# Summing the first quarter of each Strassen product in PSUM, in a four-layer graph network

## The chip, the cores and the metric

The kernel runs on one core of one Trainium2 chip. The metric is the device time of one execution in microseconds (us). The core has five engines with a queue each: TensorE (PE in the profile, with its weight loads as PEld) multiplies and writes to PSUM, an accumulator memory of eight banks of 512 float32 columns on 128 partitions; VectorE (DVE) and ScalarE (ACT) read and write PSUM and the working memory SBUF; GpSimd (POOL) works on SBUF alone; SyncE (SP) issues most of the transfers to and from DRAM.

## What is computed

128 graphs of 128 nodes with 512 features, x, and a matrix of edge weights, adj, for each graph, go through four layers. Each ends in `x = _layernorm(x + layer(x))`, which subtracts the mean over the 512 features and divides by the standard deviation. All is in float32.

- Layer 0: a transition matrix is made from adj and two scores of each node; the result is relu(x W0 + T x W1 + T T x W2 + biases).
- Layer 1: two hypergraph convolutions (512 to 1024 to 512 features), with a relu and a layer norm on the 1024 hidden features between them.
- Layer 2: an adjacency made from the sum of two node scores, row-normalised, times x, times a 512 x 512 weight.
- Layer 3: attention with 8 heads; the scores are multiplied by twice adj; then the output projection.

## The kernel before, in words

**Tiles.** Graphs go in pairs (`U = 2`), and two pairs (`both`) make one step of a layer, so a layer has 32 steps. A weight multiplication of a pair is done by one level of Strassen's scheme in Winograd's form, `strassen`: the left matrix (two graphs by the features) and the weight are cut in four, and seven products of sums of blocks take the place of eight. Where `twice` is used, a second level stands over it for two pairs: seven calls of `strassen`. A step has 29 calls: 7 in layer 0 (output width `nh` = `QW` = 386), 7 and 2 in layer 1, 2 in layer 2, 7 (queries and keys), 2 (values) and 2 (output) in layer 3, all of these 256 wide. In `twice`, two of the seven calls write fresh results; the other five add to what stands there, with `biased_take`.

**A call of `strassen`** uses three PSUM banks. `al` takes the product P1, then S2 T2 is added to it (step V), then S3 T3 (step C22), and at the end A22 N4 (step C21). `be` takes P5 (S1 T1), then S4 B22 (step C12). `ga` takes A12 B21 (step P2). After every one of the seven groups of matmuls a function of `take` reads the bank: `take["p1"]` copies P1 to the quarter d11, and `take["c11"]` adds P2 to it. In `plain_take` the first is a ScalarE copy and the second a VectorE addition; in `biased_take` both are VectorE's. A later group of matmuls on `al` waits until the reader before it is done. In `fresh` of layer 0 a read is split: ScalarE copies columns 128 on, VectorE adds a bias to the first 128.

**Layer norms.** `layer_norm` takes the statistics of one graph's rows (`bn_stats`), and `norm_terms` makes from them two columns: VectorE aggregates, adds eps to the variance and negates the mean; GpSimd raises the variance to the power -1/2 (`po.tensor_tensor(..., neghalf, OP.pow)`); ScalarE multiplies the negated mean by it. Then ScalarE applies both to the rows. There are 640 such norms.

**PSUM places.** Six places of the kind `bank` and one each of `t0` and `t1` fill the eight banks. `t0` and `t1` serve the T x steps of layer 0 (there too, ScalarE copies into PSUM and TensorE then adds to the copy, with `start=False`), and join `bank` when layer 0 no longer needs them.

**Order.** Nothing is ordered by loops. Every operation is recorded by `Plan.add` with a key (the layer's step plus the entries of `WHEN0`, `WHEN1`, `WHEN2` and the like), the operations that it depends on, and the tiles that it uses. `Plan.order` (line 250 on) then lists all engines' operations together: at each point an engine takes, of the operations that could start within `SLACK` of the soonest, the one of lowest rank, by durations from `estimate` and delays between engines from `LATENCY`. A tile gets a place when its first operation is listed; places of one kind are given in the order of a common line, and out of order only where at least four more are free. `Plan.emit` writes the order out. Since it issues all instructions itself, the profile puts every instruction on its line 373; groups are told apart by tiles and shapes. Waits between engines are put in afterwards, from what each instruction reads and writes.

**The end.** In `attention`, `last` marks the last pair of graphs: its probabilities are turned by TensorE (`pe.transpose` and a ScalarE copy), while those of all other pairs are written to DRAM by `through_dram` and read back, then turned by VectorE (`turned`).

Of the kernel before, what the change touches and what calls it, by code (L numbers as in the profile page):

```python
# [14 lines left out]
OP = mybir.AluOpType  # L15
AX = mybir.AxisListType

P = 128
# [14 lines left out]
OUTS = 3  # L33
SPACE = 3


# [31 lines left out]
SIZE = {"four": U * D, "sq": U * (P + 2), "bank": D, "col": 12, "row": D, "w28": 7168, "q7": 7 * 2 * P,  # L68
        "w7": 7 * QW, "out": U * 4 * QW, "t0": D, "t1": D, "row1": 4 * D, "k": U * (P + 2),
        "prep": U * D}  # L70

SIDE = 2
PSUM = "bank", "t0", "t1"

# [307 lines left out]
def kernel(  # L382
# [27 lines left out]
    slots = {"w7": 7, "out": OUTS, "q7": 0, "w28": 0, "sq": SQS, "col": COLS, "row": ROWS, "bank": 6, "t0": 1, "t1": 1,  # L410
             "four": BUFS, "row1": 0, "k": 0, "prep": 0}
    for kind in ("sq", "col", "row", "bank", "t0", "t1", "four"):
# [201 lines left out]
    def strassen(ops, W, nk, nh, take, more=None, flip=False):  # L614
# [21 lines left out]
        mm(al, A11, B11, True)  # L636
        take["p1"](al[:, :nh])
        be = bank()
# [3 lines left out]
        take["v"](al[:, :nh])  # L642
        ga = bank()
        mm(ga, A12, B21, True)
        if "c11" in more:
# [43 lines left out]

    def norm_terms(st, n=1):  # L690
        mv = col(2)
        ve.bn_aggr(mv, st[:, :6 * n])
        ve.tensor_scalar(mv[:, 1:2], mv[:, 1:2], EPS, None, op0=OP.add)
        ve.tensor_scalar(mv[:, 0:1], mv[:, 0:1], -1.0, None, op0=OP.mult)
        rstd = col(1)
        po.tensor_tensor(rstd, mv[:, 1:2], neghalf, OP.pow)
        nmr = col(1)
        ac.mul(nmr, mv[:, 0:1], rstd)
        return nmr, rstd

    def layer_norm(t):

        st = col(12)
        stats(st, 0, t)
        nmr, rstd = norm_terms(st)
        ac.activation(t, t, AF.Identity, bias=nmr, scale=rstd)

    def normed(take, t):

        def then(f, b):  # L710
            def run(p):
                f(p)
                layer_norm(t[:, b])
# [155 lines left out]
    def prepare0():  # L869
# [80 lines left out]
    def layer0(i0):  # L950
# [16 lines left out]
        def fresh(bs):  # L967
            def takes(d):
                def put(d, b):
                    def run(p):  # L970
                        ac.copy(d[:, P:], p[:, P:])
                        add(d[:, :P], p[:, :P], b, OP.add)
                    return run
                d11, d12, d21, d22 = d
                return plain_take(*d) | {"p1": put(d11, bs[:, 0]), "v": put(d12, bs[:, 1]),
                                         "p5": put(d22, bs[:, 1]), "c21": put(d21, bs[:, 0])}
            return takes
# [25 lines left out]
        for r, i in enumerate(both):  # L1003
            plan.key = base + WHENT[1][r]
            x0 = load_rows(x[i:i + U].rearrange("b p f -> p b f"))
            TT = pair_turned(loads[r])
            for m in (1, 0):
                for b in range(U):
# [5 lines left out]
                    if m:  # L1014
                        ac.copy(to, by)
                    else:
                        ve.scalar_tensor_tensor(x0[:, b], p, 0.0, x0[:, b], op0=OP.max, op1=OP.add)
                        layer_norm(x0[:, b])
                plan.key += .2
# [115 lines left out]
    def layer1(i0):  # L1135
# [66 lines left out]
        for r, i in enumerate(both):  # L1202
            plan.key = base + STEP1 * (5, 7)[r]
            for b in range(U):
# [4 lines left out]
                sts = col(12)  # L1209
                for g in range(2):  # L1210
                    stats(sts, g, h[r][b][:, g])
                nmr, rstd = norm_terms(sts, 2)
                ac.activation(t, t, AF.Identity, bias=nmr, scale=rstd)
                loads.append(through_dram(h[r][b].rearrange("p (j g) (k w) -> p j (g k) w", j=1, k=2), f"h{i + b}"))
        for r, i in enumerate(both):
# [14 lines left out]

            q = four()
            for b in range(U):
                ve.scalar_tensor_tensor(q[:, b], bw2, drds[r][:, b:b + 1], b2_b, op0=OP.mult, op1=OP.add)
                ve.scalar_tensor_tensor(q[:, b], x1[:, b], 2.0, q[:, b], op0=OP.mult, op1=OP.add)
            for b in range(U):
                p = bank()
                pe.matmul(p, K[:, b, :P], G[:, b], start=True, stop=True)
                ve.scalar_tensor_tensor(q[:, b], p, dns[r][b], q[:, b], op0=OP.mult, op1=OP.add)
                layer_norm(q[:, b])
            sp.dma_start(x2d[i // U], q)  # L1240
# [91 lines left out]
    def layer23(i0):  # L1332
# [64 lines left out]
        def fresh(bias):  # L1397
            def takes(d):
# [6 lines left out]
                d11, d12, d21, d22 = d  # L1405
                return plain_take(*d) | {"p1": put(d11, 0), "v": put(d12, 1), "p5": put(d22, 1), "c21": put(d21, 0)}
            return takes
# [144 lines left out]
```

## Time and profile before

| What | Value |
|---|---|
| Median of 3 runs | 5459.64 us (5459.48 to 5468.14) |
| Profiled execution | 5463.22 us; from its first to its last instruction (span) 5461.4 us |
| Instructions | 93,897 |
| TensorE busy | 5338.6 us, 98% of the span |
| VectorE busy | 4544.2 us, 83% |
| GpSimd busy | 4032.8 us, 74% |
| ScalarE busy | 2382.0 us, 44% |
| Mean granted TensorE clock | 0.994 of full |
| DRAM | 459.43 MB read, 350.09 MB written, 148 GB/s over the span |

A float32 matmul of the code is two records in the trace, and a transpose on TensorE too. Layer 0 takes the span from its start to about 1400 us, layer 1 goes to about 3100 us, layers 2 and 3 take the rest. How to read a group's line: engine, operation, the tile written, the tiles read, shapes, how many; then busy time in us and the mean of one in ns; then the idle time of the engine just before them, and who ended it. A line of waits has who waited, for whom, us in total, how often, and the longest. A line of a stretch has its ends and length, then each engine's busy time and instructions, the clock, and the share and rate of the transfers.

### The profile page before, as it was taken

To read this page: it belongs to the slowest core of one execution; us is meant where nothing else is said; L and a number is where in the kernel's file an instruction comes from. 1 tells how busy PE (TensorE), PEld (TensorE's weight loads), DVE (VectorE), ACT (ScalarE), POOL (GpSimd) and SP (SyncE) were. 2 spreads that over 40 slices of the span, in tenths; PEclk is the share of its full clock that TensorE was granted. 3 is DMA by queue.
4 is the path that set the end of the run, shared out by engine and by line. 5 is a ranking of instruction groups with operands and counts; after the bars stand their busy time and mean duration, and the time that the engine had idled before them with its cause. 6 is when DMAs were issued, how large, how long until landed. Compare 5 with 4: busy or idle time off the path is not lost.

```text
span 5461.4 us, 93897 instructions
## 1 busy us (share of the span) xinstructions
PE 5338.6 (98%) x29065; PEld 4256.9 (78%) x29065; DVE 4544.2 (83%) x11573; ACT 2382.0 (44%) x6437; POOL 4032.8 (74%) x4875
## 2 busy tenths in 40 slices
PE   8999999999999999999999999999999999999998
PEld 4555555555778888888888888998999998999987
DVE  6889888887888989998989878787787887787776
ACT  2434433344434444444444344554444444545444
POOL 6777777665777777777777567877777777777776
PEclk9999999999999999999999999999999999999999
DMA  3444444445454554554545645555555555455443
GB/s 100 134 139 125 133 143 128 128 120 162 146 149 150 145 155 150 151 157 147 154 146 150 225 139 159 167 155 157 162 154 164 156 158 161 153 163 162 153 153 123
DMA packets 841933, 815.80 MB, mean 149 GB/s; under 512 B 269388, under 2 KB 640596, under 8 KB 841431
## 3 DMA queue, kind: packets, MB, share of 16 engines
q1 hardware_dynamic: 839926, 807.18, 48.7%
q8 instruction: 230, 3.77, 0.3%
q10 hardware_dynamic: 1504, 2.62, 0.2%
q14 instruction: 273, 2.23, 0.1%
HBM read 459.43 MB, written 350.09 MB: 148 GB/s over the span
## 4 chain that ended last, share of the span: by engine, by line
PE 76%; DVE 10%; DMA 4%; POOL 3%; SPq 3%; issue 2%; ACT 1%; DVEq 0%; POOLq 0%; ACTq 0%
PE bank L373 58%; PE t L373 19%; DVE out L373 3%; DVE four L373 3%; SPq L373 3%; DVE col L373 2%; POOL four L373 1%; DVE side L373 1%; DMA sq<-in_adj_dram 1%; POOL out L373 1%; DMA first<-x3d 1%; DMA four<-in_x_dram 0%; DMA out<-x3d 0%; ACT out L373 0%; DVE sq L373 0%
## 5 line engine op out<-in xcount | busy, mean ns | idle before, releaser
L373 PE MATMUL bank<-first,four 128*128 128x386 f32 (+3 forms) x6114 | 1733.2, 430 | 58.4 <-DVE out L373 21.8
L373 PEld LDWEIGHTS bank<-first,four 128*128 128x128 f32 (+2 forms) x6114 | 1070.3, 189 | 640.1 <-DVE out L373 132.1
L373 DVE TENSOR_TENSOR out<-bank,out 128x386 f32<-128x386 f32 (+1 forms) x2030 | 981.6, 502 | 211.9 <-PE bank L373 164.2
L373 POOL TENSOR_TENSOR col<-col,neghalf 128x1 f32<-128x1 f32 x640 | 368.7, 582 | 452.1 <-DVE col L373 451.5
L373 DVE TENSOR_TENSOR four<-bank,four 128x256 f32<-128x256 f32 x1256 | 514.8, 416 | 177.5 <-PE bank L373 158.3
L373 POOL TENSOR_TENSOR out<-out 128x772 f32<-128x772 f32 (+3 forms) x250 | 350.2, 1408 | 263.2 <-DVE out L373 189.4
L373 PE MATMUL bank<-first,out 128*128 128x256 f32 (+2 forms) x2048 | 498.7, 377 | 7.5 <-DVE side L373 2.8
L373 POOL TENSOR_TENSOR four<-four 128x256 f32<-128x256 f32 (+2 forms) x439 | 357.6, 827 | 142.7 <-DVE four L373 76.1
L373 ACT COPY out<-bank 128x258 f32<-128x258 f32 (+2 forms) x527 | 214.1, 409 | 550.7 <-PE bank L373 414.2
L373 PEld LDWEIGHTS bank<-first,out 128*128 128x128 f32 (+2 forms) x2048 | 372.3, 189 | 77.3 <-issue 9.5
L373 POOL TENSOR_TENSOR four<-four,four 128x256 f32<-128x256 f32 (+2 forms) x479 | 414.0, 869 | 7.2 <-PE bank L373 1.3
L373 ACT ACTIVATE col<-col,col 128x1 f32<-128x1 f32 x640 | 183.9, 291 | 401.0 <-POOL col L373 348.5
L373 PE MATMUL bank<-first 128*128 128x128 f32 (+1 forms) x2356 | 329.6, 278 | 1.9 <-DVE four L373 1.3
L373 ACT ACTIVATE four<-four,col,col 128x512 f32<-128x512 f32 (+1 forms) x367 | 324.2, 887 | 7.4
L373 PEld LDWEIGHTS bank<-first 128*128 128x128 f32 (+1 forms) x2356 | 300.5, 189 | 18.1 <-issue 2.9
L373 PE MATMUL bank<-out,first 128*128 128x128 f32 (+2 forms) x1832 | 301.0, 305 | 1.1 <-DVE col L373 0.8
L373 ACT COPY four<-bank 128x256 f32<-128x256 f32 (+1 forms) x329 | 137.7, 422 | 355.5 <-PE bank L373 333.5
L373 DVE BATCH_NORM_STATS2 col<-four 128x6 f32<-128x512 f32 x430 | 287.6, 678 | 4.8 <-ACT four L373 3.1
L373 PEld LDWEIGHTS bank<-out,first 128*128 128x128 f32 (+1 forms) x1832 | 250.1, 187 | 19.4 <-issue 1.5
L373 PE MATMUL t<-out,sq 128*128 128x512 f32 x512 | 255.5, 594 | 6.4 <-DVE sq L373 2.5
L373 PE MATMUL bank<-four,first 128*128 128x256 f32 (+3 forms) x1424 | 253.3, 322 | 2.7 <-DVE first L373 1.1
L373 ACT COPY t<-out 128x512 f32<-128x512 f32 x256 | 151.0, 591 | 198.6 <-DVE four L373 107.2
(567 smaller groups left out, 12925.7 us busy)
## 6 DMA issues: line engine op xcount, KB each, us to landing
four<-x1d SPq DMA_DIRECT2D x69, 512.0 KB, 5.2
four<-h SPq DMA_DIRECT2D x66, 512.0 KB, 4.5
four<-in_x_dram SPq DMA_DIRECT2D x504, 64.0 KB, 2.1
h<-four SPq DMA_DIRECT2D x252, 128.0 KB, 2.6
four<-in_x_dram SPq DMA_DIRECT2D x60, 512.0 KB, 3.9
x1d<-four SPq DMA_DIRECT2D x60, 512.0 KB, 2.8
four<-S SPq DMA_DIRECT2D x50, 512.0 KB, 4.4
h<-out SPq DMA_DIRECT2D x188, 128.0 KB, 2.4
```

Source lines behind the costliest of these rows:

```text
L373: call(*map(real, args), **{n: real(a) for n, a in kw.items()})
```

## The change

**Strassen.** After P1, ScalarE copies it from `al` to the third bank, `ga`. The matmuls of P2 then go to `ga` with `start=False`, so that TensorE adds P2 to the copy. `take["p1"]` is gone, and `take["c11"]` is what `take["p1"]` was: it writes d11 in one read (a ScalarE copy in `plain_take`, one VectorE operation with the bias or the old contents in `biased_take`).

**PSUM places.** `ga` gets two places of its own, `g`, and `bank` keeps four. After layer 0 the 256-wide sums use halves of the first of these (`gh`), and the second joins `bank`. At the start every place that will be added to on top of a copy gets one matmul with `start=True`, two more than before.

**Layer norms.** The two graphs of a pair are taken together: one addition of eps on two columns, one power on two columns (GpSimd), and one product on VectorE in place of the negation there and the product on ScalarE. The norm of the first graph is applied when the statistics of the second are there.

**The end.** `last` now holds for the last two pairs.

```diff
+SEEDED = 2
-PSUM = "bank", "t0", "t1"
+PSUM = "bank", "g", "gh", "t0", "t1"
...
-    slots = {..., "bank": 6, "t0": 1, "t1": 1,
+    slots = {..., "bank": 6 - SEEDED, "g": SEEDED, "gh": 0, "t0": 1, "t1": 1,
...
+    places["gh"] = [places["g"][0][:, k * D // 2:(k + 1) * D // 2] for k in range(2)]
+    for k in range(2):
+        later["gh", k] = [("g", 0)]
+    later["bank", len(places["bank"])] = [("g", 1)]
+    places["bank"].append(places["g"][1])
...
         mm(al, A11, B11, True)
-        take["p1"](al[:, :nh])
+        ga = tile_of("g" if nh > D // 2 else "gh", nh)
+        ac.copy(ga[:, :nh], al[:, :nh])
...
-        ga = bank()
-        mm(ga, A12, B21, True)
+        mm(ga, A12, B21, False)
...
-            "p1": lambda p: ac.copy(d11, p), "c11": lambda p: add(d11, p, d11, OP.add),
+            "c11": lambda p: ac.copy(d11, p),
...
-            "p1": op(d11, b11, 0), "c11": op(d11, d11, 0), "v": op(d12, b12, 0), "c12": op(d12, d12, 0),
+            "c11": op(d11, b11, 0), "v": op(d12, b12, 0), "c12": op(d12, d12, 0),
...
+    def norm_terms(sts):
+        mv = col(2 * U)
+        for b, st in enumerate(sts):
+            ve.bn_aggr(mv[:, 2 * b:2 * b + 2], st)
+        mean, var = (mv.rearrange("p (b k) -> p k b", k=2)[:, k] for k in range(2))
+        ve.tensor_scalar(var, var, EPS, None, op0=OP.add)
+        rstd = col(U)
+        po.tensor_tensor(rstd, var, neghalf.to_broadcast([P, U]), OP.pow)
+        nmr = col(U)
+        ve.scalar_tensor_tensor(nmr, mean, -1.0, rstd, op0=OP.mult, op1=OP.mult)
+        return [(nmr[:, b:b + 1], rstd[:, b:b + 1]) for b in range(U)]
+    def layer_norms():
+        sts = []
+        def one_more(t):
+            sts.append((t, col(6)))
+            stats(sts[-1][1], 0, t)
+            if len(sts) == U:
+                for (t, _), (nmr, rstd) in zip(sts, norm_terms([st for _, st in sts])):
+                    ac.activation(t, t, AF.Identity, bias=nmr, scale=rstd)
+        return one_more
...
-        for kind in ("t0", "t1"):
-            p = tile_of(kind, D)
+        for kind, k in ("g", 0), ("g", 1), ("t0", 0), ("t1", 0):
+            p = tile_of(kind, D, place=k)
...
-        last = i0 + U == B
+        last = i0 + 2 * U >= B
```

More of the change, by code (lines that the diff above doesn't have):

```diff
@@ L68 @@
 SIZE = {"four": U * D, "sq": U * (P + 2), "bank": D, "col": 12, "row": D, "w28": 7168, "q7": 7 * 2 * P,
-        "w7": 7 * QW, "out": U * 4 * QW, "t0": D, "t1": D, "row1": 4 * D, "k": U * (P + 2),
+        "w7": 7 * QW, "out": U * 4 * QW, "t0": D, "t1": D, "g": D, "gh": D // 2, "row1": 4 * D, "k": U * (P + 2),
         "prep": U * D}
 SIDE = 2
-PSUM = "bank", "t0", "t1"
+PSUM = "bank", "g", "gh", "t0", "t1"
 class Tile:
@@ L409 @@
                                   if at("w7", i) < at(kind, k) + SIZE[kind] and at(kind, k) < at("w7", i) + SIZE["w7"]]
-    slots = {"w7": 7, "out": OUTS, "q7": 0, "w28": 0, "sq": SQS, "col": COLS, "row": ROWS, "bank": 6, "t0": 1, "t1": 1,
+    slots = {"w7": 7, "out": OUTS, "q7": 0, "w28": 0, "sq": SQS, "col": COLS, "row": ROWS, "bank": 6 - SEEDED, "g": SEEDED, "gh": 0, "t0": 1, "t1": 1,
              "four": BUFS, "row1": 0, "k": 0, "prep": 0}
-    for kind in ("sq", "col", "row", "bank", "t0", "t1", "four"):
+    for kind in ("sq", "col", "row", "bank", "g", "t0", "t1", "four"):
         places[kind] = [(psum if SIZE[kind] == D and kind != "row" else const).tile([P, SIZE[kind]], FP, name=f"{kind}{k}")
@@ L688, in stats @@
         ve.bn_stats(st[:, 6 * k:6 * k + 6], piece)
[L690 to L706, printed above, removed]
+    def norm_terms(sts):
[18 more added lines that the diff above has]
+        return one_more
     def normed(take, t):
+        norm = layer_norms()
         def then(f, b):
@@ L712, in run @@
                 f(p)
-                layer_norm(t[:, b])
+                norm(t[:, b])
             return run
@@ L974, in takes @@
                 d11, d12, d21, d22 = d
-                return plain_take(*d) | {"p1": put(d11, bs[:, 0]), "v": put(d12, bs[:, 1]),
+                return plain_take(*d) | {"c11": put(d11, bs[:, 0]), "v": put(d12, bs[:, 1]),
                                          "p5": put(d22, bs[:, 1]), "c21": put(d21, bs[:, 0])}
@@ L1006, in layer0 @@
             TT = pair_turned(loads[r])
+            norm = layer_norms()
             for m in (1, 0):
@@ L1017, in layer0 @@
                         ve.scalar_tensor_tensor(x0[:, b], p, 0.0, x0[:, b], op0=OP.max, op1=OP.add)
-                        layer_norm(x0[:, b])
+                        norm(x0[:, b])
                 plan.key += .2
@@ L1203, in layer1 @@
             plan.key = base + STEP1 * (5, 7)[r]
+            sts = []
             for b in range(U):
@@ L1208, in layer1 @@
                 ac.activation(t, t, AF.Relu)
-                sts = col(12)
+                sts.append(col(12))
                 for g in range(2):
-                    stats(sts, g, h[r][b][:, g])
-                nmr, rstd = norm_terms(sts, 2)
+                    stats(sts[b], g, h[r][b][:, g])
+            for b, (nmr, rstd) in enumerate(norm_terms(sts)):
+                t = h[r][b].rearrange("p g f -> p (g f)")
                 ac.activation(t, t, AF.Identity, bias=nmr, scale=rstd)
@@ L1231, in layer1 @@
             q = four()
+            norm = layer_norms()
             for b in range(U):
@@ L1238, in layer1 @@
                 ve.scalar_tensor_tensor(q[:, b], p, dns[r][b], q[:, b], op0=OP.mult, op1=OP.add)
-                layer_norm(q[:, b])
+                norm(q[:, b])
             sp.dma_start(x2d[i // U], q)
@@ L1405, in takes @@
                 d11, d12, d21, d22 = d
-                return plain_take(*d) | {"p1": put(d11, 0), "v": put(d12, 1), "p5": put(d22, 1), "c21": put(d21, 0)}
+                return plain_take(*d) | {"c11": put(d11, 0), "v": put(d12, 1), "p5": put(d22, 1), "c21": put(d21, 0)}
             return takes
```

## The prediction

> **What bounds the kernel now.** I began with the page's head and its chain that ended last.
>
> ```profile
> span 5461.4 us, 93897 instructions
> PE 5338.6 (98%) x29065; PEld 4256.9 (78%) x29065; DVE 4544.2 (83%) x11573; ACT 2382.0 (44%) x6437; POOL 4032.8 (74%) x4875
> PE 76%; DVE 10%; DMA 4%; POOL 3%; SPq 3%; issue 2%; ACT 1%; DVEq 0%; POOLq 0%; ACTq 0%
> ```
>
> TensorE sets the end, and VectorE is the one that most often holds it up. The 98% hides how often: each matmul is drawn with its pipeline tail, so short stalls are covered. I therefore took the distance from one matmul's start to the next. Undisturbed, it is 323 ns at 386 columns, 215 at 256, 111 at 128 and 428 at 512; the first layer's timeline shows more than that.
>
> ```profile
> 619.52 6.88 PE L373 MATMUL bank<-first,four 128*128 128x386 f32 x20
> ```
>
> That is 344 ns each. Summed over the trace (pairs with a missing record left out), starts lie 254 us later than these floors. Ordered by the step that was late: V 49 us, C22 40, C12 17, C21 68 (these four wait for a quarter of their own product to be read out of PSUM), P1 and P5 30, P2 3, other matmuls 47. The waits view names the engines:
>
> ```profile
> PEld bank L373 <- DVE out L373: 147.2, 332, 4.0
> PEld bank L373 <- DVE four L373: 37.3, 78, 4.6
> PEld bank L373 <- ACT out L373: 24.5, 42, 1.3
> ```
>
> The weight load waits for VectorE six times as long as for ScalarE. Busy times by stage (layer 0, layer 1, layers 2 and 3) say why; columns are PE, PEld, DVE, ACT, POOL.
>
> ```profile
> 100.00:1300.00 1200.00, 1180.85 (x3529) 638.84 (x3528) 1026.71 (x2572) 486.62 (x1139) 851.23 (x995) 1.00 0.44 130
> 1500.00:3000.00 1500.00, 1482.02 (x7078) 1256.16 (x7077) 1348.02 (x3380) 624.58 (x1153) 1128.06 (x1372) 1.00 0.50 150
> 3300.00:5400.00 2100.00, 2088.78 (x15482) 1901.60 (x15481) 1669.34 (x4400) 1019.15 (x3517) 1627.05 (x1995) 1.00 0.51 157
> ```
>
> VectorE is at 86%, 90% and 79%, ScalarE at 41%, 42% and 49%: one queue has little room, the other much.
>
> **What the Trainium skill says.** "Perfetto Trace Analysis", Identifying the Most-Contended Engine: matmul busy time is no measure of headroom; the 254 us under a 98% row agree. "PSUM — Partial Sum Buffer", PSUM bank collisions: two engines on one bank at once is an error, reads against reads included, so accesses to a bank must be kept apart. The trace agrees: where ScalarE and VectorE read disjoint columns of one bank, one follows the other, in all 256 such pairs of P1, V, P5 and C21, as here.
>
> ```profile
> 447.34 0.37 ACT L373 COPY out<-bank 128x258 f32<-128x258 f32 x1 [0.27 <-PE bank L373]
> 447.75 0.29 DVE L373 TENSOR_TENSOR out<-bank,row 128x128 f32<-128x128 f32 x1 [0.22 <-ACT out L373]
> ```
>
> "ScalarE: Activation LUTs", Step-by-step: what each stage is for, says ScalarE writes PSUM faster than SBUF; the trace shows no difference (591 ns to PSUM, 588 to SBUF, below), and I use the trace.
>
> **The change part by part.** The rows for prices:
>
> ```profile
> L373 DVE TENSOR_TENSOR out<-bank,out 128x386 f32<-128x386 f32 x1312 | 688.6, 550 | 141.7 <-PE bank L373 104.7 <-POOL out L373 18.3 <-ACT out L373 0.9
> L373 DVE TENSOR_TENSOR four<-bank,four 128x256 f32<-128x256 f32 x1256 | 514.8, 416 | 177.5 <-PE bank L373 158.3 <-POOL four L373 4.2 <-ACT four L373 2.6
> L373 ACT COPY four<-bank 128x256 f32<-128x256 f32 x254 | 93.5, 370 | 289.9 <-PE bank L373 271.5 <-DVE four L373 16.2
> L373 ACT COPY t<-out 128x512 f32<-128x512 f32 x256 | 151.0, 591 | 198.6 <-DVE four L373 107.2 <-PE bank L373 69.5 <-DVE out L373 8.7
> L373 ACT COPY out<-t 128x512 f32<-128x512 f32 x155 | 91.1, 588 | 106.6 <-PE t L373 104.7 <-DMA h<-side 1.6
> L373 POOL TENSOR_TENSOR col<-col,neghalf 128x1 f32<-128x1 f32 x640 | 368.7, 582 | 452.1 <-DVE col L373 451.5
> L373 ACT ACTIVATE col<-col,col 128x1 f32<-128x1 f32 x640 | 183.9, 291 | 401.0 <-POOL col L373 348.5 <-DVE col L373 47.2 <-POOL sq L373 1.5
> L373 DVE TENSOR_SCALAR col<-col 128x1 f32<-128x1 f32 x1280 | 134.4, 142 | 2.8
> ```
>
> There are 32 passes of 7+7+2+2+7+2+2 = 29 products, 928 in all: 224 of 386 columns, 704 of 256. Each loses one VectorE addition, biased or plain, and gains one ScalarE copy. VectorE: 224 x 0.55 + 704 x 0.416 = 416 us less. ScalarE: 224 x 0.48 (between 370 at 256 and 590 at 512) + 704 x 0.37 = 368 us more. No matmul is added; the first-quarter group only starts without clearing.
>
> The 640 norms become 320 pairs. ScalarE loses 184 us. VectorE loses 134 us of small scalings and gains 320 additions and 320 products at some 0.15 us, 96: 38 less. GpSimd loses 640 powers and gains 320 on two columns. No row shows that width: between the one-column 0.58 (183 us saved) and twice that (nothing saved); I take 0.65, 160 saved. Sums: DVE 4544 - 454 = 4090 (75%), ACT 2382 + 184 = 2566 (47%), POOL 3870 (71%). None is the bound, so nothing of this counts directly; what counts is the 254 us.
>
> *V, 49 us.* V overwrites the bank from which P1 is read. In 608 of 928 products that read was a VectorE addition (0.55 or 0.42 us) behind a queue at 79 to 90%; now it is a 0.48 or 0.37 us copy on an engine below 55%. In layer 0's other 64 it was a copy and an addition one after the other, 0.37 + 0.03 + 0.29 us, now one copy. Half goes: -25 (bounds -40, and +10 if copies queue behind norms and exponentials).
>
> *C22, C12, C21, 125 us.* Their releasers stay on VectorE, mostly; its demand falls a tenth, and its queue with it. I take 30% off: -38 (bounds 0 and -65).
>
> *P1, P5 and the rest, 80 us.* They wait for transposes and sums on VectorE and GpSimd, both lighter, but about 26 us of it is the start, which is DMA and preparation: -8 (0 to -20).
>
> *P2 as filler.* In 452 products P2 was issued ahead of V, filling the wait for the P1 read. Now P2 needs the copy too. On the old times 305 of them would wait, 86 us together, if nothing took their place. The bank order eases here: the third bank leaves the common line, so the next product's P1 and P5 can come earlier, and V already starts a median 2.0 us (256 columns) after P1. I take +15 (0 to +86).
>
> *Banks.* Layer 0 keeps four common banks instead of six. Without the third bank, products and transposes held over four for 29 us of its 1400, exactly four for 365: +12 (0 to +40). Later the seeded sums of two products are halves of one bank, which the old times would have made meet 79 times for 18 us, almost all on ACT or DVE: +4 (0 to +18).
>
> *Start and end.* Two more opening matmuls of 512 columns (two passes of 0.43): +2. The penultimate pair of graphs turns its probabilities on TensorE instead of through DRAM. It adds 32 passes x 0.11 = 3.5 us and four copies of 0.59, and takes away two stores and two loads on SP and the wait for them. In the trace both last attentions are late together, and TensorE sits idle:
>
> ```profile
> 5430.68 1.12 PE L373 MATMUL bank<-ident,first 128*128 128x128 f32 x4 [6.33 <-POOL first L373]
> ```
>
> The new transposes and the earlier context fit into that hole, but the copies (2.4 us) stand in the last softmax's queue: -4. The first norm of the last pair waits for the second, one 0.8 us pass more at the end: +1. Net -3 (-7 to +3).
>
> Sum: -25 - 38 - 8 + 15 + 12 + 4 + 2 - 3 = -41. The profiled execution took 5463.2 us, 2 us around its span, and gives 5422; the median of the runs, 5459.6, is 3.6 lower, so the forecast is **5418 us**.
>
> **Rivals.** *A larger gain.* If VectorE's lag behind the written order is nearly all of the trouble, V and its followers lose two thirds of 175 us and the new waits stay near 10: about 5350. For it: VectorE's rows are long and dense in layer 1. Against: starts, stage changes and the tail (near 70 of the 254) remain. *No change.* The 30% and 50% come out at half (-40) while filler and banks take 40: 5460. For it: the order is made anew, and TensorE has other work in its queue for most reads. *Slower.* One mechanism: P2 loses its place as filler, at the 305 places where it stood between P1 and V. It decides once more than some 70 of its 86 us are really lost; at the full 86 it gives 5459.6 - 41 + 71 = 5490. Against: one to three products are in flight at once. *The change doesn't do what it says*: if the compiled order still read P1 on VectorE, nothing would move; the diff leaves no such read.
>
> **How the numbers follow.** Forecast's case 64% (5375 to 5445), larger gain 9%, no change 16% (a third of it past -0.2%), slower 11%. Runs of this kernel agree within about 0.2%, 11 us, so that bound separates the answers: faster 0.64 + 0.09 + 0.05 = 0.78, same 0.11, slower 0.11. The range 5372 to 5466 leaves out the larger gain and most of the slower case.
>
> **What would show it.** Right: VectorE near 4090 us and ScalarE near 2570; the waits of weight loads for VectorE down by a third or more; V's lateness halved; those for ScalarE up, from 25 to perhaps 45; no idle of 6 us near the end. Wrong: weight loads waiting for ScalarE by 100 us or more at V and P2, or new gaps before P1 in layer 0 with no read late (banks). A ScalarE copy from bank to bank that takes far more than 0.37 us would also break it.

## The result, and the profile after

The changed kernel takes 5539.48 us (median of 4 runs, 5535.08 to 5542.16) against 5459.56 us before on the same chip: a ratio of 1.0143, 95% interval [1.0126, 1.0161]. It is 80 us slower; 5418 us was forecast. The granted clock is 0.994 in both profiles.

The head of the page and its chain that ended last, after:

```profile
span 5533.3 us, 92639 instructions
PE 5392.1 (97%) x29085; PEld 4256.4 (77%) x29085; DVE 4342.2 (78%) x10003; ACT 2541.9 (46%) x6729; POOL 3982.9 (72%) x4555
PE 77%; DVE 9%; DMA 5%; ACT 3%; issue 2%; POOL 2%; SPq 1%; DVEq 0%; ACTq 0%; POOLq 0%
```

VectorE did lose work (4544 to 4342 us) and ScalarE gained what was forecast (2542, forecast 2570). Neither helped: TensorE still sets the end and is now less well fed. The three stretches, with the columns as in the prediction, show where:

```profile
100.00:1300.00 1200.00, 1177.79 (x3513) 638.59 (x3513) 941.38 (x2236) 550.38 (x1220) 826.33 (x934) 1.00 0.45 129
1500.00:3000.00 1500.00, 1462.43 (x6922) 1220.15 (x6921) 1297.05 (x2849) 620.92 (x1154) 1105.57 (x1243) 1.00 0.48 147
3300.00:5400.00 2100.00, 2082.95 (x15226) 1872.20 (x15223) 1581.58 (x3738) 1068.38 (x3615) 1589.20 (x1848) 1.00 0.50 156
```

The count of matmul records in a stretch of fixed length is a throughput. It falls from 3529 to 3513 in layer 0, from 7078 to 6922 (2.2%) in layer 1 and from 15482 to 15226 (1.7%) in layers 2 and 3. The ends of the stages agree: the last product of layer 0 ends 3 us later than before, and all that follows takes 69 us more. The waits of the weight loads name the engines:

```profile
PEld bank L374 <- DVE out L374: 122.7, 256, 5.3
PEld g L374 <- ACT g L374: 54.3, 139, 2.4
PEld bank L374 <- ACT out L374: 35.4, 37, 6.9
...
PEld bank L374 <- DVE four L374: 23.7, 44, 4.0
...
PEld bank L374 <- ACT g L374: 17.3, 45, 1.0
```

The two lines for VectorE are shorter than before (122.7 for 147.2, and 23.7 for 37.3). Against that stand the new waits for ScalarE's copy (`g <- ACT g`: P2 waits for it; `bank <- ACT g`: V does), 72 us together.

Counted as in the prediction, by starts later than the undisturbed distance, TensorE's lateness grew from 254 to 323 us, 69 us of a span that is 72 us longer. By step: V from 49 to 37, C22 40 to 64, C12 17 to 22, C21 68 to 69, P1 and P5 30 to 25, P2 3 to 53, other matmuls 47 to 53.

### The profile page after: what moved, and what is told of

Read it like the earlier page. It is cut to its first block, busy times and chain, and to the rows that moved or that the text cites. A ratio compares the mean times of both kernels' runs of the same rounds, so it can differ in the third digit from the quotient of the medians.

```text
span 5533.3 us, 92639 instructions
## 1 busy us (share of the span) xinstructions
PE 5392.1 (97%) x29085; PEld 4256.4 (77%) x29085; DVE 4342.2 (78%) x10003; ACT 2541.9 (46%) x6729; POOL 3982.9 (72%) x4555
## 4 chain that ended last, share of the span: by engine, by line
PE 77%; DVE 9%; DMA 5%; ACT 3%; issue 2%; POOL 2%; SPq 1%; DVEq 0%; ACTq 0%; POOLq 0%
PE bank L374 43%; PE t L374 18%; PE g L374 17%; DVE out L374 3%; DVE col L374 2%; DVE four L374 2%; DMA four<-in_x_dram 1%; ACT g L374 1%; DMA first<-x3d 1%; SPq L374 1%; ACT first L374 1%; DVE side L374 1%; DMA side<-x3d 1%; ACT out L374 1%; POOL first L374 1%
## 5 line engine op out<-in xcount | busy, mean ns | idle before, releaser
L374 PE MATMUL bank<-first,four 128*128 128x386 f32 (+2 forms) x4472 | 1406.8, 446 | 45.4 <-DVE out L374 25.6
L374 PEld LDWEIGHTS bank<-first,four 128*128 128x128 f32 (+1 forms) x4472 | 813.9, 190 | 539.8 <-DVE out L374 110.7
L374 DVE TENSOR_TENSOR out<-bank,out 128x386 f32<-128x386 f32 (+1 forms) x1379 | 685.6, 507 | 286.1 <-PE bank L374 227.6
L374 ACT COPY g<-bank 128x256 f32<-128x256 f32 (+1 forms) x628 | 250.6, 399 | 770.7 <-PE bank L374 700.3
L374 POOL TENSOR_TENSOR col<-col,neghalf 128x2 f32<-128x2 f32 x320 | 253.7, 796 | 374.0 <-DVE col L374 367.7
L374 PE MATMUL g<-first,four 128*128 128x256 f32 (+2 forms) x1368 | 427.0, 416 | 7.5 <-DVE four L374 2.1
L374 PEld LDWEIGHTS g<-first,four 128*128 128x128 f32 (+1 forms) x1368 | 253.3, 190 | 111.5 <-ACT g L374 19.0
L374 DVE TENSOR_TENSOR four<-bank,four 128x256 f32<-128x256 f32 x458 | 189.9, 416 | 96.3 <-PE bank L374 82.6
L374 PE MATMUL t<-first,four 128*128 128x256 f32 (+2 forms) x944 | 230.2, 370 | 4.3 <-DVE four L374 1.8
L374 PE MATMUL bank<-four,first 128*128 128x128 f32 (+3 forms) x1492 | 216.6, 292 | 2.0 <-ACT g L374 2.0
```

What stands on the lines that cost most here:

```text
L374: call(*map(real, args), **{n: real(a) for n, a in kw.items()})
```

## The experiments

Eighteen kernels were run. "Lateness" is the count just named, in each kernel's profiled run. Each ratio is against the kernel before on the same chip; chips differ by a few us, so a difference between two kernels in the text is good to some 5 us.

| Kernel | Median us | Ratio, 95% interval |
|---|---|---|
| e1, seeded sums alone | 5508.3 | 1.0089 [1.0074, 1.0104] |
| e2, pairs of norms alone | 5512.0 | 1.0106 [1.0077, 1.0135] |
| e14, the new end alone | 5463.7 | 1.0007 [1.0000, 1.0014] |
| e7, before with one bank fewer after layer 0 | 5530.1 | 1.0131 [1.0116, 1.0147] |
| e3, changed, two whole banks for the sums | 5565.4 | 1.0188 [1.0171, 1.0205] |
| e4, changed, one half bank | 5578.8 | 1.0216 [1.0201, 1.0232] |
| e6, e1 and the planner told of shared halves | 5508.2 | 1.0097 [1.0082, 1.0112] |
| e9, seeded sums in common banks | 5483.5 | 1.0035 [1.0025, 1.0045] |
| e15, e9 with ScalarE's PSUM reads planned longer | 5493.8 | 1.0064 [1.0046, 1.0082] |
| e10, seeded sums in layer 0 alone | 5432.1 | 0.9937 [0.9922, 0.9952] |
| e5, e2 with measured durations in the planner | 5488.0 | 1.0059 [1.0044, 1.0074] |
| e12, e2 with the product on GpSimd | 5506.3 | 1.0075 [1.0060, 1.0090] |
| e13, only the power by pairs | 5422.4 | 0.9932 [0.9917, 0.9947] |
| e8, changed, planner told both | 5492.8 | 1.0076 [1.0059, 1.0093] |
| e17, changed, only the power by pairs | 5480.8 | 1.0030 [1.0018, 1.0041] |
| e18, e10 and e13 together | 5449.4 | 0.9974 [0.9966, 0.9983] |
| e11, control: a planner delay by 1 ns | 5464.8 | 1.0002 [0.9993, 1.0010] |
| e16, control: e15's planner edit on before | 5467.1 | 1.0004 [0.9998, 1.0011] |

### The parts one by one

**e1**: before, with everything of the seeding and nothing else.

```diff
+        ga = tile_of("g" if nh > D // 2 else "gh", nh)
+        ac.copy(ga[:, :nh], al[:, :nh])
...
-        mm(ga, A12, B21, True)
+        mm(ga, A12, B21, False)
```

> The first quarter summed in PSUM as in the changed kernel; layer norms one by one and only the last pair turned on TensorE, as before. Theories: (H) the two halves of one shared PSUM bank after layer 0 hold up P2 and ScalarE's queue; (N) in the paired norms VectorE's queue now waits for GpSimd's power; (F) P2 lost its place as filler between P1 and V. H and F put nearly all of the 80 us here: 5520 to 5540. N puts it in the norms: 5450 to 5480 here.

**e2**: before, with the pairs of norms alone.

```diff
-        ve.tensor_scalar(mv[:, 1:2], mv[:, 1:2], EPS, None, op0=OP.add)
-        ve.tensor_scalar(mv[:, 0:1], mv[:, 0:1], -1.0, None, op0=OP.mult)
...
+        ve.tensor_scalar(var, var, EPS, None, op0=OP.add)
+        rstd = col(U)
+        po.tensor_tensor(rstd, var, neghalf.to_broadcast([P, U]), OP.pow)
+        nmr = col(U)
+        ve.scalar_tensor_tensor(nmr, mean, -1.0, rstd, op0=OP.mult, op1=OP.mult)
```

> The kernel before with the layer norms by pairs alone. N: 5490 to 5520 (VectorE idle for GpSimd's power, the reads of the sums late). H and F: 5450 to 5465, since VectorE, ScalarE and GpSimd all have less to do.

**e14**: before, with `last` for two pairs.

```diff
-        last = i0 + U == B
+        last = i0 + 2 * U >= B
```

> The kernel before with the last two pairs' probabilities turned on TensorE in place of the last one's alone. As forecast: 3 to 7 us faster, 5453 to 5460. If the ScalarE copies in the last softmax's queue weigh more: 5460 to 5468.

Measured: +49, +53 and at most +8 us. Both halves of the change lose, each for itself; the new end is worth nothing that can be measured. The two losses come to 102 us where the whole loses 80, so they overlap. Each half has to be explained.

### Why the seeded sums lose: in part a bank

The change takes the third bank of a product out of the common line. After layer 0 the kernel before has eight common banks; the changed one has seven, with one bank cut in halves for the seeded sums. **e3** gives them two whole banks (six common), **e4** one half only.

```diff
-    places["gh"] = [places["g"][0][:, k * D // 2:(k + 1) * D // 2] for k in range(2)]
+    places["gh"] = [places["g"][k][:, :D // 2] for k in range(2)]
...
-        later["gh", k] = [("g", 0)]
-    later["bank", len(places["bank"])] = [("g", 1)]
-    places["bank"].append(places["g"][1])
+        later["gh", k] = [("g", k)]
```

> The changed kernel, but after layer 0 each of the two seeded sums has a whole bank, so six common banks are left in place of seven. H: TensorE's lateness at P2 falls from 53 us to some 10 and the time to 5480 to 5500. F and N: no gain, 5530 to 5545. If scarce common banks are the cause: slower than the changed kernel, 5550 to 5570.

```diff
-    places["gh"] = [places["g"][0][:, k * D // 2:(k + 1) * D // 2] for k in range(2)]
-    for k in range(2):
+    places["gh"] = [places["g"][0][:, :D // 2]]
+    for k in range(1):
```

> The changed kernel, but after layer 0 one half bank alone holds seeded sums, one product at a time, with seven common banks as in the changed kernel. H: no two products meet in that bank, 5490 to 5515 (less overlap of products costs some of the gain). F and N: at best as the changed kernel, 5540 to 5560.

Both are slower than the changed kernel, by 26 and 39 us. The weight loads' waits of e3 show that what was won at P2 was lost elsewhere:

```profile
PEld bank L374 <- DVE out L374: 163.7, 264, 6.0
...
PEld bank L374 <- DVE four L374: 36.5, 70, 1.7
...
PEld bank L374 <- ACT g L374: 15.5, 44, 1.2
```

No `g <- ACT g` stands among the twelve longest waits any more: P2's lateness fell from 53 to 4 us. But the waits for VectorE's reads rose from 122.7 and 23.7 to 163.7 and 36.5, and C21's lateness from 69 to 126. With one common bank fewer, the wait stands at another step and is longer. e3 thus changes two things at once, the halves and the count of common banks. So I took the bank from the kernel before, and nothing else (**e7**): `t1` no longer joins the common banks after layer 0.

```diff
-    for kind in ("t0", "t1"):
+    for kind in ("t0",):
```

> The kernel before, but with seven common banks after layer 0 in place of eight (one stays unused). K: 5490 to 5520, the third bank of each product is sorely missed. H and B: 5455 to 5475.

Its stretches of layer 1 and of layers 2 and 3:

```profile
1500.00:3000.00 1500.00, 1469.54 (x7011) 1233.76 (x7010) 1359.16 (x3340) 608.28 (x1141) 1135.79 (x1354) 1.00 0.50 149
3300.00:5400.00 2100.00, 2062.09 (x15131) 1863.65 (x15130) 1668.56 (x4329) 1008.03 (x3434) 1613.26 (x1957) 1.00 0.50 155
```

And the waits of its weight loads:

```profile
PEld bank L373 <- DVE out L373: 172.7, 357, 4.0
PEld bank L373 <- issue: 156.5, 632, 4.9
PEld bank L373 <- DVE four L373: 53.8, 96, 2.0
PEld bank L373 <- DVE first L373: 35.0, 30, 12.8
```

One bank out of eight, with no other edit, costs 75 us by the medians on that chip (1.0131). The throughput falls from 7078 to 7011 and from 15482 to 15131 records. The waits for VectorE are those of before, longer (147.2, 37.3 and 13.0 then): the same queue hurts more where fewer results can stand and wait for it. By step, C22 and C21 grew by 14 and 12 us, but most of the growth, from 47 to 100 us, is at the other matmuls, the transposes and the products outside `strassen`; a single gap of 12.45 us near the end, before the matmul at 5492.6 us, is part of it. The 75 us price the kernel before, whose products take all three banks from the common line. In the changed kernel a product takes two of them there, so its price for the bank can be another. "Perfetto Trace Analysis", Optimization Strategy, of the Trainium skill says that gaps which repeat on the engine that should be full can mean too few buffers in SBUF or PSUM; here the measurement agrees, and no row of the profile says "bank", because the wait is put down to the reader that empties one.

**e6**: the planner of e1 does not know that accesses of two engines to the two halves of a bank are kept apart; here it is told.

```diff
+                if split[k]:
+                    t = max(t, *(halves[f] + LATENCY[f][e] for f in range(5) if f != e))
```

> The seeding alone, and the planner told that accesses of different engines to the two halves of the shared bank come one after the other. If meeting halves are what the order doesn't foresee (H): TensorE's lateness at P2 from 36 us to under 10, the time from 5508 to 5470 to 5490. If banks as such are short (K): 5500 to 5515.

P2's lateness went from 36 to 6 us and the time did not move (5508.3 and 5508.2); C21's went from 70 to 95. A wait was cured and came back elsewhere. Nor was it all that e1 lost by. Its weight loads have three long waits that the kernel before does not have:

```profile
PEld bank L374 <- DVE four L374: 38.6, 59, 13.6
...
PEld bank L374 <- POOL sq L374: 16.3, 5, 15.6
...
PEld t L374 <- DVE sq L374: 11.6, 4, 10.4
```

The last number of each line is its longest wait. On TensorE they are gaps of 15.2, 10.0 and 13.2 us, where layer 1 and layer 2 begin and near the end (before the matmuls at 1369, 3132 and 5463 us); the longest gap of the kernel before is the 6.33 us near its end. e6 has all three too. They make up 39 us of e1's lateness, which grew from 254 to 296. The matmuls there wait for operands that GpSimd and VectorE prepare; that the missing bank brought these gaps about is not shown. **e9** sets no bank aside: the seeded sum goes to a common bank. This kernel leaves out the opening matmul that the changed kernel gives each of its places `g`, and P1 is missing from part of its sums. So it prices the bank and is no kernel to use. The same holds for e15 below.

```diff
-        take["p1"](al[:, :nh])
+        ga = bank()
+        ac.copy(ga[:, :nh], al[:, :nh])
```

> The seeding alone, but the third bank comes from the common banks as before (six in layer 0, eight later), so nothing is set aside and no bank is shared by two sums. [...] Seeing to it that P2 depends on the copy is all that is left. If the loss of the seeding is in banks (K, H): 5450 to 5470. If it is in P2's lost place as filler (F) or in ScalarE's load: 5495 to 5515.

It loses some 20 us where e1 lost 49, so what is set aside in e1, halves and missing bank together, goes with some 28 us; the three long gaps are gone too (none here passes 8 us). P2 waits for a copy here as well, and its lateness is 3 us: it is the halves of one bank, not the copy, that made P2 late in e1. Layer 0 ends 14 us earlier than before; the loss lies behind it. Was it the planner's belief that a ScalarE read of PSUM is shorter than it is? **e15** lengthens it.

```diff
-        return 50 + n / 1.2 + (0 if psum else 43) + 92 * scalars + 94 * ("accum_out" in kw)
+        return 50 + n / 1.2 + (107 if psum else 43) + 92 * scalars + 94 * ("accum_out" in kw)
```

> The seeding with the third bank from the common ones[...], and the planner told that a ScalarE read of PSUM takes 107 ns longer than it reckons (256 columns: 370 for 263). Belief: from 5484 to 5440 to 5465. F (P2 behind the copy): 5475 to 5490.

No: 5493.8 against 5483.5. What costs 25 to 35 us in layers 1 to 3 without a bank set aside is not settled. By step, C21's lateness in e9 is 88 us for 68 before and that of the other matmuls 61 for 47; ScalarE's added copies in these layers and the order made anew are both left as causes.

**e10**: seeding in the 386-wide products of layer 0 alone, where the sums have two places `g` and four banks stay common, as in the changed kernel; all eight banks are common afterwards.

```diff
+        seeded = nh > D // 2
+        if seeded:
+            ga = tile_of("g", D)
+            ac.copy(ga[:, :nh], al[:, :nh])
+        else:
+            take["p1"](al[:, :nh])
...
+    for k in range(2):
+        later["bank", len(places["bank"])] = [("g", k)]
+        places["bank"].append(places["g"][k])
```

> The seeding in layer 0 alone, with four common banks and two for the sums; after it all eight banks are common and the first quarter is read twice, as before. Norms as before. In the run with the seeding everywhere layer 0 ended 10 us sooner than before. K: 5440 to 5455. F: 5460 to 5475.

5432.1 us, 30 less than before on its chip. Layer 0 ends 11 us earlier: there the idea works as meant. Layers 1 to 3 are 20 us shorter too, although their code is as before; that part can only come from the order that the planner makes. Against e9, on the same chip and also with eight common banks after layer 0, leaving the 256-wide products unseeded is worth 51 us. So the seeding behind layer 0 loses in these runs even where no bank is set aside, and the bank is one part of it.

### Why the pairs of norms lose: two columns in SBUF take VectorE's shared port

In e2, the groups by shape give for the scaling and the product on VectorE:

```profile
L373 DVE TENSOR_SCALAR col<-col 128x2 f32<-128x2 f32 x384 | 99.7, 261 | 3.3
L373 DVE SCALAR_TENSOR_TENSOR col<-col,col 128x2 f32<-128x2 f32 x320 | 79.1, 249 | 38.0 <-POOL col L373 37.6
```

The same in the changed kernel, with GpSimd's power before them:

```profile
L374 POOL TENSOR_TENSOR col<-col,neghalf 128x2 f32<-128x2 f32 x320 | 253.7, 796 | 374.0 <-DVE col L374 367.7 <-DVE cols L374 1.9
L374 DVE TENSOR_SCALAR col<-col 128x2 f32<-128x2 f32 x384 | 109.1, 285 | 4.1
L374 DVE SCALAR_TENSOR_TENSOR col<-col,col 128x2 f32<-128x2 f32 x320 | 103.1, 326 | 37.0 <-POOL col L374 36.9
```

(64 of the 384 scalings belong to other work.) A two-column step took 249 to 326 ns, where 150 was forecast and one column takes 142. The mean hides two kinds. Sorted by whether a GpSimd instruction ran at the same time, those of the changed kernel are: the scaling 156 ns without (197 of them) and 421 with (187); the product 148 without (173) and 536 with (147). The one-column scalings of the kernel before took 142 ns without (436) and 141 with (844), and none of the 1280 passed 300. Of the 164 long ones (over 300 ns) after, 156 end within 50 ns of the end of a GpSimd instruction. One of them in the timeline:

```profile
198.27 1.82 POOL L374 TENSOR_TENSOR out<-out 128x772 f32<-128x772 f32 x1
...
198.75 0.30 DVE L374 BATCH_NORM_AGGREGATE col<-col 128x2 f32<-128x6 f32 x2
...
199.09 1.02 DVE L374 TENSOR_SCALAR col<-col 128x2 f32<-128x2 f32 x1
...
200.12 0.56 DVE L374 TENSOR_TENSOR out<-bank,out 128x386 f32<-128x386 f32 x1
```

The scaling of two columns starts at 199.09 while GpSimd adds 772 columns, and ends at 200.11, 0.02 us after that addition (198.27 + 1.82 = 200.09). Behind it on VectorE stands the read of a product, `out<-bank,out`, which empties a bank. "SBUF — State Buffer", Who interferes with whom, of the Trainium skill states it: VectorE's second pair of ports to SBUF is GpSimd's too; a `tensor_scalar` in a two-port mode takes it, and who comes second waits for the whole of the other's instruction; an instruction with two SBUF inputs contends for it with a GpSimd instruction that reads SBUF. "VectorE: DVE Perf Modes", Mode 2×_2P — use both read ports for one tensor, wants operands in SBUF whose outermost dimension longer than one is even, or odd and equal in source and destination: two columns can be split over two ports. That a single column cannot is my reading of it. The trace agrees for the scaling, 142 and 141 ns with one column, 156 and 421 with two, and for the product, 148 and 536. The kernel has a function, `shares_port`, that says the same of every operation and by which the planner lists such steps apart from GpSimd's; the prediction left it out.

The profile of before already had this case, twice over:

```profile
L373 DVE TENSOR_SCALAR col<-col 128x2 f32<-128x2 f32 x64 | 21.7, 339 | 0.0
...
L373 DVE TENSOR_SCALAR col<-bank 128x2 f32<-128x2 f32 x51 | 6.7, 132 | 1.1 <-PE bank L373 0.6 <-ACT ks L373 0.3
```

The 64 two-column scalings of other work took 158 ns without GpSimd beside them (29) and 489 with (35). The 51 that read their two columns from PSUM took 132 ns with GpSimd beside them (47). So it is not the width alone: it is two columns that lie in SBUF.

**e5** tells the planner these durations.

```diff
+        if n == 2 and name in ("tensor_scalar", "scalar_tensor_tensor"):
+            return 285 if name == "tensor_scalar" else 326
-        return 500 + 35 * n if OP.pow in args else 150 + 2.1 * n if n < 800 else 1.82 * n
+        return (796 if n == 2 else 535) if OP.pow in args else 150 + 2.1 * n if n < 800 else 1.82 * n
```

> The layer norms by pairs alone, and the planner told what the paired steps take in the trace (two-column scaling 285 ns, product 326, power 796, where it reckons some 68, 68 and 570). If the written order is wrong because it takes that chain for half as long (B, belief): from 5512 back to 5455 to 5475. If it is the steps' own time on VectorE, up 60 us with them (W, work): 5500 to 5515.

24 us came back, though the long two-column steps became more (211 for 146). So nearly half of the loss depends on the order, made on too short durations in e2, and the waits at the port are not a cost one for one. **e12** takes the product to GpSimd, so that VectorE no longer waits for the power, but has two two-column scalings to a pair.

```diff
+        ve.tensor_scalar(mean, mean, -1.0, None, op0=OP.mult)
-        ve.scalar_tensor_tensor(nmr, mean, -1.0, rstd, op0=OP.mult, op1=OP.mult)
+        po.tensor_tensor(nmr, mean, rstd, OP.mult)
```

> The layer norms by pairs alone, with the product of mean and deviation on GpSimd right behind its power (VectorE negates the means before it), so VectorE's queue no longer waits for the power (37.6 us in the run with the pairs alone). If that wait is the loss: from 5512 to 5465 to 5485. If it is the dearer small steps and the planner's belief: 5500 to 5515.

It still loses 44 us on its chip, where e2 lost 53. The 38 us of `<-POOL col` in e2's line was not the main part; the norms' steps that take the port are still 640, and two-column scalings again take 158 ns without GpSimd beside them and 409 with. **e13** keeps VectorE's steps at one column and the products on ScalarE, and pairs only the power.

```diff
+        for b, st in enumerate(sts):
+            m = mv[:, 2 * b:2 * b + 2]
+            ve.bn_aggr(m, st)
+            ve.tensor_scalar(m[:, 1:2], m[:, 1:2], EPS, None, op0=OP.add)
+            ve.tensor_scalar(m[:, 0:1], m[:, 0:1], -1.0, None, op0=OP.mult)
...
+        for b in range(U):
+            ac.mul(nmr[:, b:b + 1], mv[:, 2 * b:2 * b + 1], rstd[:, b:b + 1])
```

> The kernel before with the power alone taken for both graphs of a pair; VectorE's scalings stay one column each and ScalarE makes the products for each graph, so VectorE gets no longer steps. If the two-column steps' time on VectorE is the loss (W): 5450 to 5470. If it is that the first graph's norm waits for the second (P): 5490 to 5515.

Its groups of the power and of the scalings, by shape:

```profile
L373 POOL TENSOR_TENSOR col<-col,neghalf 128x2 f32<-128x2 f32 x320 | 249.8, 781 | 258.6 <-DVE col L373 254.7 <-DMA e<-sq 3.2
...
L373 DVE TENSOR_SCALAR col<-col 128x1 f32<-128x1 f32 x1280 | 133.5, 143 | 5.0
```

5422.4 us: 38 less than before, 90 less than e2, and the fastest of all these kernels. The 1280 scalings take 143 ns again, and the power by pairs saves GpSimd 119 us (368.7 to 249.8). The pairing was never the trouble; VectorE's two-column steps were.

### Both halves together

**e8**: the changed kernel with the planner told of the halves (e6) and of the durations (e5).

> The changed kernel with the planner told both things. If B and H explain the loss: 5450 to 5490. If W and K do: 5525 to 5545.

5492.8 us: some 40 less than the changed kernel, and still 37 over before. **e17**: the changed kernel with e13's norms.

```diff
-        ve.tensor_scalar(var, var, EPS, None, op0=OP.add)
+            ve.tensor_scalar(m[:, 1:2], m[:, 1:2], EPS, None, op0=OP.add)
+            ve.tensor_scalar(m[:, 0:1], m[:, 0:1], -1.0, None, op0=OP.mult)
...
-        ve.scalar_tensor_tensor(nmr, mean, -1.0, rstd, op0=OP.mult, op1=OP.mult)
+        for b in range(U):
+            ac.mul(nmr[:, b:b + 1], mv[:, 2 * b:2 * b + 1], rstd[:, b:b + 1])
```

> The changed kernel with the norms' small steps on VectorE one column at a time again and their products on ScalarE, as in the kernel before; only GpSimd's power keeps its two columns; all the seeding stays. If the two halves of the change act by themselves, this takes back what the runs showed between the pairs alone and the power alone (5512.0 against 5422.4, 90 us): 5539 - 90 = 5450, within 5435 to 5475. If the bank set aside, ScalarE's copies and the extra small steps of ScalarE get in each other's way, it stays at 5500 or more. Between the two the loss of the whole is shared between both.

5480.8 us, 59 less than the changed kernel. The expectation of 90 was too high, but most of the 80 us goes with the two-column steps alone. What is left against before, 18 us, is what the parts say: 49 (e1) + 4 (e14) - 38 (e13) = 15. By stage it is 7 us gained in layer 0 and 24 lost after it, where the bank is missing. By step, V's lateness is 19 us (49 before) and that of C22, C12 and C21 together 95 (125 before). P2's rose from 3 to 71.

**e18**: e10 and e13 in one kernel.

> The kernel before with the seeding in layer 0 alone (all eight banks common afterwards) and GpSimd's power on two columns; nothing else of the change. Each alone gained: 30 us and 38 us. If the gains add: 5392 to 5402. If both drew on the same idle time of TensorE in layer 1 (each ended that stage some 23 to 25 us earlier than before), less than their sum: 5405 to 5425. A time above 5432 would say that one takes the other back.

5449.4 us, 14 less than before: the gains of 30 and 38 do not add, and one takes most of the other back. In the profiled run layer 0 gains 6 us and the rest 10. I have no cause for it. It bounds what these runs can say: two edits that gain alone can lose 54 us of their sum through the order made anew. The 75 us of the bank in the kernel before and the 59 and 90 us of the port stand above that, the 59 only just. The 20 us in the unchanged layers of e10, the 28 between e1 and e9, the 51 between e9 and e10 and the 26 of e3 do not.

### Two controls

**e11** and **e16** change only the planner's beliefs in the kernel before, so that it is ordered anew with the same work (in e11, 1545 of some 7500 TensorE operations change place).

```diff
-LATENCY = ((0, 205, 215, 255, 300), (225, 120, 110, 200, 200), (160, 145, 140, 200, 200), (110, 140, 100, 105, 200),
+LATENCY = ((0, 206, 215, 255, 300), (225, 120, 110, 200, 200), (160, 145, 140, 200, 200), (110, 140, 100, 105, 200),
```

> The kernel before with one of the planner's delays (TensorE to VectorE) taken as 206 ns in place of 205: nothing changes but the written order, in which a fifth of TensorE's operations change place. What differs from before is what re-planning alone can do: within 10 us if the other theories' numbers are to mean anything; if 30 us or more, a good part of every difference here may be such luck.

> Control for e15: the kernel before with the same word to the planner. ScalarE has slack and fewer copies here: 5450 to 5470 under both theories.

Neither moves the time: 1.0002 and 1.0004. Twice a new order of this work cost nothing. That is no rule: e5 has the work of e2 in another order and gains 24 us, layers 1 to 3 of e10 have the work of before and gain 20, and e18 loses 54 us of a sum.

## Why the prediction was wrong

**V, -25.** Half came: -12 in the whole change. In e1 and e9, without the pairs, it was -23 and -25, and in e2, with the pairs alone, +12. The step and its price were right (the copy took 361 ns at 256 columns and 467 at 386, against 0.37 and 0.48).

**C22, C12, C21, -38.** This failed: together they went from 125 to 155 us, +29. I reasoned from VectorE's total to its queue, and the runs do not follow that total. With 272 and 244 us less of it they are 121 us in e1 and 157 in e9; with the total of before, 91 in e13 (4554 us busy, 4544 before) and 151 in e7 (4595). The growth in the changed kernel goes with the two-column steps: C22, 40 before and in e1, is 86 in e2, 64 in the changed kernel and 45 in e17. Banks count as well (e7, e3), but e9, with all of them common, shows that they are not the whole. In e17 the three are 95, near the forecast, but e13 has 91 with nothing seeded, so that is no proof of the reasoning. That VectorE's total fell less than forecast (4342 for 4090) has two causes. The additions went as counted: 704 of 256 columns and 224 of 386, 411 us of durations in e1. But VectorE's page share fell by only 272 there. Records of successive VectorE instructions overlap by some 70 to 85 ns, so that an instruction taken out frees less than its duration, and VectorE's other instructions, above all those with two inputs of 512 columns, took some 40 us more. The other cause is the next step.

**Layer norms: the small steps "at some 0.15 us".** This is the step of the prediction that failed most clearly, by mechanism and not by size alone. 0.15 is right for two columns beside an idle GpSimd (156 and 148 ns) and wrong beside a running one (421 and 536), and GpSimd runs three quarters of the time. The page's busy time of these two groups is 109.1 + 103.1 us, some 20 of it of other work, against the 96 forecast. Taking the steps out of the changed kernel gives back 59 us (e17). I priced a width and did not ask what the instruction shares: the price had no term for a wait behind GpSimd. The power took 796 ns, between the bounds (582 and twice that) but above my 650.

**Banks, "+4 (0 to +18)" for what comes after layer 0.** This is the other step that failed. I priced how often two halves would meet and gave no price at all to the bank that is no longer common. e7 puts that bank at 75 us in the kernel before, and e3 another one at 26 in the changed kernel; halves and bank together are 28 us between e1 and e9 with the sums seeded. That is the figure that belongs to this change. The other 25 to 35 us that seeding costs behind layer 0 (e9) had no term in the prediction either, and their cause stays open. Layer 0's own +12 was no worse than forecast: in e1 the last layer-0 product ends 10 us earlier than before.

**P2 as filler, +15 (0 to +86).** P2's lateness did rise by 51 us, inside the bounds. But waiting for the copy is not why: e9 waits for it too and P2 is 3 us late. The halves of one bank are, and with P2 down to 4 and 6 us nothing was gained in e3 and e6. Both changed something else with it (a bank, the order), so what P2's lateness alone costs is not shown. The slower rival (5490) had the sign; that P2 was late was right, the reason it gave was not.

**P1, P5 and the rest, -8; the end, -3.** 77 us of lateness before and 78 after; e14 measures +4 us [0, +8] for the end. TensorE's idle time before the transposes of the last attentions shrank from 6.33 to 2.08 us, and nothing measurable came of it.

**Two readings of the lines** were off, without bearing on the sum. The "no difference" between ScalarE's copies to PSUM and to SBUF compared 591 ns out of SBUF with 588 ns out of PSUM; with PSUM as the source of both, 256 columns take 361 ns to PSUM and 370 to SBUF. And on the lines shown weight loads waited seven and a half times as long for VectorE as for ScalarE (147.2 + 37.3 against 24.5), not six.

**The range**, 5372 to 5466, left out the slower rival and reached no case in which something shared became scarcer. Both steps that failed lacked a bound for a resource that two users share: the banks, and the port that VectorE shares with GpSimd.

## What to carry to other kernels

Before an accumulator bank is set aside, take one bank away from the kernel as it is, with no other edit: that warns of what banks are worth, and here it was 75 us of 5460. What the bank costs in the new kernel takes a run of its own (28 us here, e1 against e9). Before small steps are joined, ask which shared port the wider form takes; sort its durations by what the other engine does at that moment, since a mean of 285 ns was 156 and 421. The profile at hand may have the wider form already, as this one did. A wait that a profile names (P2 for its copy) is not yet a cost: cure it alone first, because with the true limit left in place it stands at the next step.

## What the runs showed of the hardware

- A VectorE scaling of one column in SBUF takes 142 ns whether GpSimd runs or not; of two columns in SBUF 156 ns alone and 421 ns beside GpSimd, the long ones ending some 25 ns (median) after GpSimd's instruction; of two columns in PSUM 132 ns beside GpSimd.
- GpSimd's power on two columns takes a median of 707 ns against 549 on one (means 796 and 582).
- Successive VectorE records overlap by some 70 to 85 ns (median 82 in the kernel before): a 142 ns step in a dense queue holds the next start back by a median of 61 ns (1077 cases).
- A ScalarE copy of 256 columns out of PSUM takes 361 ns to PSUM and 370 to SBUF.
